# A graph network on one core: in the sort of the edges, ScalarE's copy of the running numbers is emitted one batch after VectorE's running sum

## Chip, cores and metric

The kernel runs on one core of one Trainium2 chip. The metric is the time of one execution on the device in microseconds; lower is better. A core has five engines with a queue each: PE (TensorE, matmuls; its weight loads are listed as PEld), DVE (VectorE), ACT (ScalarE), POOL (GpSimd) and SP (SyncE, which here issues the DMAs).

## What is computed

Two graph networks run one after the other on 6250 nodes with 128 features; the 206,250 edges (two directions of 100,000, and one loop for each node) come sorted by target. The first network gathers both ends of each edge, passes them through a small network and sums by target, in two layers. The second averages the neighbours, in three.

```python
for l in range(n_layers):                       # 2, first network
    m = jnp.concatenate([h[row], h[col]], axis=-1)
    m = jax.nn.relu(m @ msg_W1[l].T + msg_b1[l])
    m = m @ msg_W2[l].T + msg_b2[l]
    agg = jax.ops.segment_sum(m, col, num_segments=h.shape[0])
    upd = jnp.concatenate([h, agg], axis=-1) @ upd_W[l].T + upd_b[l]
    h = _layer_norm(h + upd, ln_g[l], ln_b[l])
...
for i in range(NUM_LAYERS):                     # 3, second network
    agg = jax.ops.segment_sum(h[src], dst, num_segments=n) * inv_deg
    h = agg @ Wl[i].T + bl[i] + h @ Wr[i].T
```

## The kernel before

Nodes are padded to 49 blocks of 128 (`NB`). Gathers and sums are matmuls with matrices of zeros and ones that are built on the chip.

**The sort.** For each target block `w`, the generator `sort(w)` takes a window of 36 x 128 edges and gives each edge of the block a place among 128 slots of its source block. It is cut into steps by `yield`; a `next` on the iterator `ahead` emits one step. The steps in order, with the lines of the profile:

1. load of the window `ed` (L333)
2. `key` (L336) and the one-hot `oh` over source blocks (L339), on VectorE
3. sums over quarters `half`, `four` (L343, L345) and the totals `tot` (L348), on VectorE
4. two small matmuls that give the start of each partition's count (L351, L352), and their copy by ScalarE into `four` (L353)
5. the running sum on VectorE (L356), then ScalarE's copy of it into the upper quarter of `upper` (L359) and VectorE's subtraction into the lower (L360)
6. `run` (L363 to L365), 7. `rank` (L368), 8. `fit`, `own`, `over`, `place` (L371 to L378), 9. `lo` and `v` (L384 to L386), all on VectorE
10. to 12. six `pick` tiles, two a step (helper L88, VectorE)
13. to 15. 36 matmuls of `pick` and `v` into the bank `so`, twelve a step (L398)
16. two copies of that bank by ScalarE, `sv` (L403) and `sv_f` (L405)
17. a transpose on TensorE (L408), ScalarE's copy `sv_t` (L410), and its store to the table `svd` in memory (L411)

That is 17 steps. `ed` has three buffers, `key` and `tot` two, and `oh`, `half`, `four`, `upper`, `run` and `v` one each.

**The loop around it.** In each of the two layers each target block is worked in 13 batches (`NI`) of four source blocks; the last batch holds source block 48 and the block's second part. In a batch `i` of layer 0 these are emitted, in this order:

- `fetch`, four batches ahead: a broadcast load `v_all` of a part of `svd[w]` (L430)
- the pending stores (L618): the one-hots to `ohd`, the counts to `cnt`
- `hot_first`, two batches ahead: VectorE builds `hot` (two operations, helper L88, three buffers) from `sv[w]` and `ot` (L442, four buffers) from `v_all`
- `picked`: 24 matmuls with `ot` into a `pe` bank (L501, L503), and ScalarE's `m` from it (L508)
- `widened`: ScalarE's `hd` from `hot` (L458)
- `settle`: the matmuls `agg` of the batch before (L521); after a block's last batch also the first step of `update`, which copies `agg` out by ScalarE (L530)
- `counts`: four matmuls into the one bank `pa` (L466), ScalarE's copy `ca` (L468), and in two batches of a block a further copy `kept` (L473, L480)
- a step of `update` of the block before, in every second batch (its last ones give `rest` at L210 and the matmul L232)
- one step of `ahead`, two in batches 2, 5, 8 and 11: 17 a block
- at batch 8 (`NI - 5`), as many steps more as it takes to have the next block's table `sv[w + 1]`
- at batch 7, `target_rows` of the next block: a matmul (L237), its sum `b` with a bias on VectorE (L239), and its split in three parts by ScalarE (L209) and VectorE (L210 to L212)

So in the steady state step 1 of a sort is emitted at batch 9 of one block, step 5 at batch 12, step 6 at batch 0 of the next block and steps 16 and 17 at batch 8. Dependencies and waits are put in by the framework, and each engine's instructions are laid out by it when the program is built.

Layer 1 has the same loop without `sort` and `counts`; the second network then works from the stored counts alone.

The lines that give a block its steps:

```python
                    for _ in range(2 if i % 3 == 2 else 1):
                        next(ahead, None)
                    while i == NI - 5 and l == 0 and w + 1 < NB and w + 1 not in sv:
                        next(ahead)
```

Of the kernel before, what the change touches and what calls it, by code (L numbers as in the profile page):

```python
# [67 lines left out]
def fast(tc, dram, ident, miss_i, x, src, dst, weights, columns, rows, out, edges):  # L68
# [12 lines left out]
    with ExitStack() as ctx:  # L81
# [247 lines left out]
        def sort(w):  # L329
# [24 lines left out]
            yield  # L354
            num, last = (four[:, x].rearrange("p k c -> p (k c)") for x in range(2))
            nc.vector.tensor_tensor_scan(last, num, num, 0.0, OP.add, OP.bypass)  # L356
            last = four[:, 1, :, 1:].rearrange("p k c -> p c k")
            upper = early.tile([128, H, NB], F16, name="upper", bufs=1)
            nc.scalar.copy(upper[:, Q:], last)  # L359
# [210 lines left out]
        def settle(most):  # L570

            nonlocal behind
            while len(pending) > most:
# [4 lines left out]
                if cols[-1] == NB:  # L578
# [3 lines left out]
                    next(behind)  # L582

        ahead = (None for w in range(NB) for _ in sort(w))
        while 0 not in sv:
            next(ahead)
# [345 lines left out]
```

## Time and profile before

| | |
|---|---|
| median of 3 runs | 4183.11 us (4173.44 to 4191.63) |
| the profiled execution's own time | 4183.25 us |
| its span, first to last instruction | 4181.5 us, TensorE's granted clock 0.987 |
| layer 0, from the first to the last running sum of the sort (L356) | 104.0 to 1896.9 us |
| TensorE busy in 400 to 800 us (layer 0) | 375.81 us of 400 |
| VectorE busy there | 337.26 us |
| ScalarE busy there | 252.46 us |
| running sum L356, copy L359, subtraction L360 | 1172, 989 and 949 ns, 49 of each |
| copies `sv` L403 and `sv_f` L405 | 621 and 569 ns, 49 of each |
| transpose L408, copy `sv_t` L410 | 276 and 277 ns |
| matmul L398 of the sort | 208 ns, 1764 of them, overlapped |

Durations of single instructions overlap with those of their neighbours on the same engine, so the distance from start to start is often less than the duration. In a line of the timeline the first two numbers are start and duration in us, then engine, line, operation, what it writes and reads, and in brackets the idle time of the engine before it and what ended it.

### The profile page before, as it was taken

How to read it: one execution, taken by the hardware profiler on the slowest of the kernel's cores; microseconds unless marked ns; L12 is line 12 of the kernel's file. 1: busy time of each engine (PE TensorE's matmuls, PEld its weight loads, DVE VectorE, ACT ScalarE, POOL GpSimd, SP SyncE). 2: the span in 40 equal slices, each digit the busy share in tenths (PEclk: the TensorE clock that was granted, in tenths of full speed). 3: DMA queues.
4: the chain of work that ended last, by engine and by line, in shares of the span. 5: the costliest groups of instructions: out<-in, count | busy, mean ns of one | idle time of the engine just before them, and what ended most of it. 6: DMA issues, size and time to landing. Idle time of an engine off the chain costs nothing. (4 is left out here: it accounts for less than half of the span.)

```text
span 4181.5 us, 118306 instructions
## 1 busy us (share of the span) xinstructions
PE 3971.0 (95%) x46833; PEld 3697.7 (88%) x46833; DVE 2935.0 (70%) x6941; ACT 2493.0 (60%) x4673; POOL 63.4 (2%) x59
## 2 busy tenths in 40 slices
PE   4899999999999999999999999999999999999998
PEld 2899999999999999999999999999999888888887
DVE  6888888888888888886777777777776444444443
ACT  4566666666666666666666666666665555555554
POOL 6000000000000000000000000000000000000000
PEclk8899999999999999999999999999999999999999
DMA  2455554555445545455666666666665444443554
GB/s 82 144 154 149 160 157 152 149 162 159 150 152 159 159 151 157 153 162 173 197 197 197 199 198 200 200 199 198 199 199 176 130 128 118 129 128 111 161 153 121
DMA packets 656082, 671.18 MB, mean 161 GB/s; under 512 B 113200, under 2 KB 504474, under 8 KB 655386
## 3 DMA queue, kind: packets, MB, share of 16 engines
q1 hardware_dynamic: 655514, 663.51, 53.0%
q8 instruction: 368, 6.03, 0.6%
q14 instruction: 200, 1.64, 0.1%
HBM read 534.28 MB, written 128.99 MB: 159 GB/s over the span
## 5 line engine op out<-in xcount | busy, mean ns | idle before, releaser
L501 PE MATMUL pe<-a,ot 128*128 128x128 bf16 x14700 | 1635.0, 221 | 1.5 <-DVE ot L442 1.4
L503 PE MATMUL pe<-b,ot 128*128 128x128 bf16 x14700 | 1631.2, 220 | 0.0
L501 PEld LDWEIGHTS <-ot 128*128 128x128 bf16 x14700 | 1033.9, 98 | 27.4 <-DVE ot L442 2.5
L503 PEld LDWEIGHTS <-ot 128*128 128x128 bf16 x14700 | 1037.5, 98 | 0.6
L695 PE MATMUL pe<-cf,h 128*128 128x512 f32 (+1 forms) x3822 | 926.5, 394 | 3.5 <-issue 1.9
L442 DVE TENSOR_SCALAR ot<-v_all,part 128x1024 bf16<-128x1024 bf16 (+1 forms) x1274 | 597.9, 472 | 321.7 <-PE pe L503 178.7
L695 PEld LDWEIGHTS pe<-cf,h 128*128 128x128 f32 x3822 | 676.1, 189 | 143.6 <-issue 2.0
L521 PE MATMUL agg<-m,hd 128*128 128x129 f32 x4900 | 694.6, 284 | 21.3 <-ACT agg_s L530 20.8
L689 ACT CAST cf<-c 128x2048 fp32r<-128x2048 uint8 (+2 forms) x253 | 433.6, 1714 | 340.7 <-PE pe L695 283.3
L521 PEld LDWEIGHTS agg<-m,hd 128*128 128x128 f32 x4900 | 603.8, 193 | 28.8 <-ACT agg_s L530 28.4
L88 DVE TENSOR_TENSOR hot<-sv,iota 128x512 bf16<-128x512 f16 (+1 forms) x1274 | 476.6, 410 | 147.1 <-ACT m L508 98.7
L512 ACT ACTIVATE m_r<-pe 128x512 fp32r<-128x512 f32 (+1 forms) x637 | 369.2, 580 | 338.3 <-PE pe L503 334.5
L689 DVE CAST cf<-c 128x2048 fp32r<-128x2048 uint8 (+2 forms) x254 | 280.7, 1105 | 358.2 <-PE pe L695 213.8
L458 ACT CAST hd<-hot 128x512 f32<-128x512 bf16 (+1 forms) x637 | 383.8, 602 | 219.3 <-PE agg L521 120.8
L508 ACT ACTIVATE m<-pe 128x512 f32<-128x512 f32 (+1 forms) x637 | 377.4, 592 | 222.8 <-PE pe L503 222.4
L513 DVE SCALAR_TENSOR_TENSOR m_r<-pe,m_r 128x512 fp32r<-128x512 f32 (+1 forms) x637 | 425.8, 669 | 67.5 <-ACT m_r L512 39.5
L521 PE MATMUL agg<-m_r,hd_r 128*128 128x256 f32 x2450 | 447.6, 303 | 1.4 <-DVE m_r L513 1.1
L489 ACT CAST hd_r<-hd_b 128x512 fp32r<-128x512 bf16 (+1 forms) x637 | 383.8, 603 | 22.3 <-PE agg L521 11.1
L468 ACT CAST ca<-pa 128x512 uint8<-128x512 f32 (+1 forms) x637 | 359.5, 564 | 1.6 <-PE pa L466 1.5
L521 PEld LDWEIGHTS agg<-m_r,hd_r 128*128 128x128 f32 x2450 | 331.9, 190 | 8.8 <-DVE m_r L513 1.6
L466 PE MATMUL pa<-hot 128*128 128x128 bf16 x2450 | 247.1, 221 | 92.9 <-ACT kept L480 90.1
L466 PEld LDWEIGHTS <-hot 128*128 128x128 bf16 x2450 | 193.7, 98 | 109.6 <-issue 101.5
(152 smaller groups left out, 2989.4 us busy)
## 6 DMA issues: line engine op xcount, KB each, us to landing
v_all<-svd SPq DMA_DIRECT2D x1176, 256.0 KB
c<-cnt SPq DMA_DIRECT2D x216, 512.0 KB
ohd<-hot SPq DMA_DIRECT2D x588, 128.0 KB
hd_b<-ohd SPq DMA_DIRECT2D x588, 128.0 KB
cnt<-ca SPq DMA_DIRECT2D x540, 64.0 KB
v_all<-svd SPq DMA_DIRECT2D x98, 128.0 KB
xw<-in_x SPq DMA_DIRECT2D x49, 64.0 KB
ohd<-hot SPq DMA_DIRECT2D x49, 64.0 KB
```

The costliest lines, as they stand in the source:

```text
L88: nc.vector.tensor_tensor(to, v.rearrange("p (r e) -> p r e", e=2).unsqueeze(2).to_broadcast([B, n, B, 2]), iota_2.unsqueeze(1).to_broadca ...
L442: nc.vector.tensor_scalar(t[:, :n].rearrange("p j k s -> p (j k) s"), v[:, :2 * n], part, None, op0=OP.is_equal)
L458: nc.scalar.copy(hd[:, :n].rearrange("p (r e) v -> p r e v", e=2), hot[:, 1, :n // 2].rearrange("p r v e -> p r e v"))
L466: nc.tensor.matmul(pa[:, j * B:(j + 1) * B], hot[:, 0, j // 2, :, j % 2], hot[:, 1, j // 2, :, j % 2], start=True, stop=True)
L489: nc.scalar.copy(hd[:, :n].rearrange("p (r e) v -> p r e v", e=2), h[:, :n * B].rearrange("p (r v e) -> p r e v", v=B, e=2))
L501: nc.tensor.matmul(pe[:, o], t[:, j, 0, :], a3[l][:, block, k, :], start=(k == 0), stop=False)
L503: nc.tensor.matmul(pe[:, o], t[:, j, 1, :], b3[:, k, :], start=False, stop=(k == 2))
L508: nc.scalar.activation(m[:, :n, :D], pe, AF.Relu)
L513: nc.vector.scalar_tensor_tensor(m[:, :n, 1, :], pe, 0.0, m[:, :n, 0, :].bitcast(F32), op0=OP.max, op1=OP.subtract)
L521: nc.tensor.matmul(agg[:, :F], hd[:, j, :], v, start=(c == 0), stop=(c == NB))
L689: (nc.scalar.copy if turn % 2 else nc.vector.tensor_copy)(cf[:, :k, :n].rearrange("p s w d -> p w s d"), c8[:, :n, s % R:s % R + k])
L695: nc.tensor.matmul(p[:, :n * B], h2[l % 2][:, s, k, :], cf[:, s % K, :n].rearrange("p w d -> p (w d)"), start=(s == 0 and k == 0), stop=(s ...
```

## The change

One `yield` is added in `sort`, between the running sum and its two readers. The running sum is then a step of its own, and ScalarE's copy and VectorE's subtraction come with the next `next`. The sort has 18 steps after it; the number of steps that the loop grants is not changed.

```diff
             num, last = (four[:, x].rearrange("p k c -> p (k c)") for x in range(2))
             nc.vector.tensor_tensor_scan(last, num, num, 0.0, OP.add, OP.bypass)
+            yield
             last = four[:, 1, :, 1:].rearrange("p k c -> p c k")
             upper = early.tile([128, H, NB], F16, name="upper", bufs=1)
             nc.scalar.copy(upper[:, Q:], last)
             nc.vector.tensor_sub(upper[:, :Q], last, half[:, Q:])
             yield
```

## The prediction

> **What bounds the kernel now.** I read the page's busy table first. TensorE is busy 95% of the span, so the first thought is that only TensorE's idle time can be won.
>
> ```profile
> PE 3971.0 (95%) x46833; PEld 3697.7 (88%) x46833; DVE 2935.0 (70%) x6941; ACT 2493.0 (60%) x4673; POOL 63.4 (2%) x59
> ```
>
> The sort runs only in layer 0 (scans L356 from 104.0 to 1896.9 us), so I then took the view of waits for 200 to 1900 us.
>
> ```profile
> DVE ot L442 <- DMA v_all<-svd: 120.4, 122, 3.4
> ACT upper L359 <- DVE four L356: 118.4, 45, 4.5
> PE pa L466 <- ACT kept L480: 88.8, 45, 3.1
> PE agg L521 <- ACT agg_s L530: 17.5, 32, 1.9
> ```
>
> The obvious reading: once per node block ScalarE stands 2.6 us (118.4/45) for the scan, the copies of pa behind it come late, the one pa bank stays full, and TensorE loses 88.8/45 = 1.97 us. The changed line is the head of that chain. Before pricing it at 2 us a block I asked what sets the period of a block, with VectorE's timeline of one block (scan ends at 954.83 and at 991.89).
>
> ```profile
> 953.66 1.17 DVE L356 TENSOR_TENSOR_SCAN four<-four 128x490 f16<-128x490 f16 x1
> ...
> 978.25 0.62 DVE L348 TENSOR_REDUCE tot<-four 128x49 f16<-128x441 f16 x1
> 978.77 0.48 DVE L442 TENSOR_SCALAR ot<-v_all,part 128x1024 bf16<-128x1024 bf16 x1
> 979.17 0.75 DVE L88 TENSOR_TENSOR hot<-sv,iota 128x512 bf16<-128x512 f16 x2
> 979.84 0.28 DVE L210 TENSOR_TENSOR rest<-mm,a 128x128 f32<-128x128 f32 x1
> 980.04 0.28 DVE L239 TENSOR_TENSOR b<-mm,row 128x128 f32<-128x128 f32 x1
> ...
> 987.89 0.49 DVE L442 TENSOR_SCALAR ot<-v_all,part 128x1024 bf16<-128x1024 bf16 x1 [1.44 <-DMA v_all<-svd]
> ...
> 990.32 0.49 DVE L442 TENSOR_SCALAR ot<-v_all,part 128x1024 bf16<-128x1024 bf16 x1 [0.33 <-DMA v_all<-svd]
> 990.72 1.17 DVE L356 TENSOR_TENSOR_SCAN four<-four 128x490 f16<-128x490 f16 x1
> ```
>
> The busy sums of the three stretches of that block (columns: stretch, length, PE, PEld, DVE, ACT, POOL, clock, DMA share, GB/s):
>
> ```profile
> 954.84:980.32 25.48, 23.74 (x341) 23.24 (x341) 25.45 (x62) 16.48 (x35) 0.00 (x0) 1.00 0.47 145
> 980.32:982.94 2.62, 2.62 (x41) 2.60 (x39) 2.08 (x9) 2.47 (x7) 0.00 (x0) 1.00 0.25 81
> 982.94:991.90 8.96, 8.79 (x127) 8.58 (x125) 4.48 (x11) 4.78 (x10) 0.00 (x0) 1.00 0.74 224
> ```
>
> There is a ring. From the end of a scan to the end of b L239 VectorE has 25.45 us of work in 25.48 us: no gap. Then ScalarE, which waits for that b, works off its queue, the sorted table is stored (svd L411) and the next block's broadcasts of it (v_all) land; VectorE waits for them at three ot (1.44, 0.45 and 0.33 us; the second stands in the left-out lines), and the scan stands behind the third. ScalarE and the store:
>
> ```profile
> 980.35 0.30 ACT L209 CAST b<-b 128x128 bf16<-128x128 f32 x1 [1.82 <-DVE b L239]
> ...
> 981.55 0.59 ACT L468 CAST ca<-pa 128x512 uint8<-128x512 f32 x1
> 982.03 0.28 ACT L410 CAST sv_t<-mm 100x128 bf16<-100x128 f32 x1
> ...
> 982.95 0.35 SPq L411 DMA_DIRECT2D svd<-sv_t  x1
> ```
>
> I took the same three marks for 46 blocks from the timeline: scan end to b end 25.49 us on average (25.3 to 26.2), b end to the svd issue 2.64 (2.62 to 2.94), svd issue to the next scan's end 9.61 (8.4 to 11.0, the loads' spread). The sum is the mean period, 37.75 us. TensorE has 35.16 us of work in the block shown: its 1.9 us stall is the slack of this ring, not its cause.
>
> **What the Trainium skill says.** "TensorE: Matmul & The Clock Gate", section "Architectural detail", has ScalarE's and VectorE's queues as strict FIFO; the trace agrees, since ca L468 of the last batch (pa ready at 989.89) runs at 992.82, behind upper L359. "Perfetto Trace Analysis", section "Optimization Strategy", says to find the gaps on the limiting engine and what ends them; taken alone that leads to the ScalarE wait, and here the gapless VectorE stretch decides. Its "Summary: the profiler window per engine type" says that a queue DMA's movement is outside its window: svd L411 shows 0.35 us, while the first ot that needs it starts 4.94 us after its issue.
>
> **The change, part by part.** No instruction is added or removed. The sort gets 18 steps where the loop grants 17 a block, so the `while` at batch NI-5 = 8 gives the missing one.
>
> 1. The copy L359 and the subtraction L360 are emitted a batch later. Each engine's order in the trace is not the order of emission but what was ready: key for the last block runs at 1806.1 us, its oh at 1878.6; L359 already stands ahead of ca L468 and kept L480, which are emitted before it. ScalarE has nothing else ready between m of the last batch (989.05) and that place, so I expect L359 to stay there. Gain 0. If it does move behind m and agg_s of the next batch, TensorE gets up to 1.97 + 17.5/45 = 2.4 us a block from its stalls, yet the ring holds no part of this wait, so again 0 in the sum. The last three blocks show it: there L359 runs behind kept (1898.11, wait 0.48) and their periods are 37.9 to 38.1. Bounds 0 and 2.1 us; I take 0.
>
> 2. The three groups of twelve matmuls L398 (0.70 us a group) go from batches 5, 6, 7 to 6, 7, 8. TensorE has no gap there, so they can't be pulled forward. It comes to the matmuls L232 and L237 for rest and b one group earlier, 0.7 us. What VectorE puts before rest is filling for the next block (oh, half, four, tot), taken while it had nothing better. With rest ready 0.7 us sooner, tot (0.62) and one ot (0.48) should fall behind b, where VectorE has 5.7 us idle a block. Gain in the 25.49 stretch: between 0 and 0.62 + 0.48 + 1.11 (four L345, at 977.10, too) = 2.2; I take 1.10.
>
> 3. sv and sv_f (L403, L405) cannot run before the last group now. Today they fill ScalarE's gap at 977.83, outside the ring; then they come after ca at 981.55. From its 982.14 end: both copies 0.7, the transpose L408 0.28 with the hand-overs about 0.15, sv_t 0.28, issue: near 983.5 instead of 982.95. Loss 0.55. The first block, which today makes up five steps at that batch, bounds it: matmuls end 150.08, svd at 152.50, that is 2.42; on the 982.14 above it gives 984.5, loss 1.6. Lower bound 0.3, if SP's wait behind ohd (982.53) swallows part. TensorE's transpose stands behind the copy, and the matmuls of batch 9 behind it: about 1 us of stall, paid out of the 1.9 us of slack. If that slack were gone, it would cost that 1 us.
>
> 4. SP issues the same DMAs; svd L411 passes at most one cnt and one ohd store (0.34, 0.38). The v_all loads follow svd by the same 9.61, as the scan stays behind the third ot. Bounds: 0.49 + 0.33 = 0.8 gain if that ot falls behind the scan, 0.4 loss if another store goes first. I take 0.
>
> 5. run, rank, v and picks also move a batch. They stay in the gapless stretch, whose sum does not change by order. Picks end about 971.7 for a group at 973.6 then: covered.
>
> Sum a block: -1.10 + 0.55 = -0.55 us. Some 47 periods: -26 us. The profiled execution (span 4181.5, its time 4183.25) becomes 4157; the median shown is 4183.11, so it is 4157 there too. Layer 1 and the matrix stage have no sort.
>
> **Rivals.**
> A, gain and loss cancel (rest comes only 0.5 us earlier, or ScalarE's delay is 1.1): 4183 - 5 = 4178. For: TensorE's stall has been shown to be slack. Against: two opposite parts would have to be equal.
> B, slower: the svd tail. The copies, the transpose and the store come into the ring and nothing leaves the gapless stretch. At 0.3 to 1.6 a block, say 0.9: 47 x 0.9 = 42, 4225. It decides as soon as less than 0.55 us of filling goes behind b. For: the first block's 2.42 us tail. Against: L237 does come a group earlier.
> C, the plain reading: ScalarE's wait goes and VectorE's ring loosens as well (L360 and run behind the hot tiles, third ot behind the scan), so that TensorE's work bounds: 35.16 + 0.45 against 37.75, 2.1 us x 47 = 100, 4083. For: 118.4 us of waits in plain sight. Against: the last three blocks.
> That the order on ScalarE does not change at all is part of the forecast.
>
> **How the numbers follow.** Forecast (4130 to 4170) 0.40, of which 0.02 lies within 0.5%; A 0.23, B 0.28, C 0.09. Range: C's nearest part and the ends of step 2 (-2.2 + 0.3 = -1.9 x 47 = -89, 4094) to B's upper middle (+1.1 x 47 = 52, 4235): 4094 to 4235; the forecast's own is 4130 to 4170. 0.5% is 21 us, about what a measurement can tell from no change: faster 0.38 + 0.09 = 0.47, same 0.02 + 0.23 = 0.25, slower 0.28.
>
> **What would show it.** Right: L359 still ahead of the last ca with a wait near 2.5 us; groups L398 in batches 6 to 8; fewer fillings before rest; scan to b near 24.4, b to svd near 3.2, svd to scan near 9.6. Wrong: L359 without a wait and TensorE's L466 stall gone with a shorter period (C), scan to b still 25.5 (B), or a tail over 4 us.

## The result, and the profile after

The kernel after the change takes 4218.41 us (median of 5 runs, 4210.31 to 4220.93), the kernel before 4183.11 us. The ratio is 1.0082 with a 95% interval of 1.0061 to 1.0104: slower, and the whole interval lies above the 0.5% that the prediction took for what a measurement can tell from no change. Forecast was 4157. The profiled execution has a span of 4208.5 us (4181.5 before) and a granted clock of 0.991 (0.987).

The page's busy table looks as before; the work is the same.

```profile
PE 3964.9 (94%) x46833; PEld 3684.6 (88%) x46833; DVE 2931.5 (70%) x6941; ACT 2503.0 (59%) x4673; POOL 63.2 (2%) x59
```

The view of waits for 200 to 1900 us, the layer with the sort (us in total, times, longest):

```profile
PE mm L409 <- ACT sv_f L406: 74.3, 44, 2.2
ACT upper L360 <- DVE four L356: 70.6, 42, 3.1
...
DVE ot L443 <- DMA v_all<-svd: 62.3, 81, 1.9
...
PE pa L467 <- ACT kept L481: 42.7, 43, 2.4
...
PE agg L522 <- ACT agg_s L531: 23.3, 40, 1.1
```

Lines below the new `yield` have moved by one. ScalarE's wait for the scan fell from 118.4 to 70.6 us and TensorE's wait at `pa` from 88.8 to 42.7 us. A reader who stops there would call the change a success. In their place stands a wait that was not there, 74.3 us at the transpose L409, and the whole is longer.

The periods say where. I measured the same marks in 45 blocks of each timeline, in us after the end of a scan L356 (means):

| | before | after |
|---|---|---|
| period, scan end to scan end | 37.74 | 38.45 |
| second matmul group for b, L237, ends | 23.35 | 22.72 |
| b L239 starts on VectorE | 25.21 | 25.23 |
| VectorE ends the hot pair (two `hot` operations in a row) that feeds the next `ohd` store | 27.69 | 27.70 |
| VectorE's idle time up to there | 0.15 | 0.21 |
| transpose starts | 25.73 | 27.99 |
| `sv_t` ready | 27.56 | 28.61 |
| store `svd` issued | 28.14 | 28.66 |
| from there to the end of the next scan | 9.60 | 9.78 |
| the third ot on the new table, the last before the scan, starts | 36.17 | 36.25 |
| from its start to the start of that scan | 0.40 | 1.02 |
| TensorE's idle time in a period | 2.38 | 3.19 |

The period grew by 0.70 us: 0.52 up to the store and 0.18 behind it. Over 47 periods that is 33 us, against the 34 us that the ratio gives (0.0082 x 4183). The two profiled executions themselves differ by 27.0 us: from the first to the last scan the changed one is 31.8 us longer, and the rest of it is 4.8 shorter.

Now one block of the changed kernel (its scan ends at 585.10). VectorE's timeline:

```profile
608.75 0.62 DVE L348 TENSOR_REDUCE tot<-four 128x49 f16<-128x441 f16 x1
609.27 0.76 DVE L88 TENSOR_TENSOR hot<-sv,iota 128x512 bf16<-128x512 f16 x2
609.94 0.30 DVE L210 TENSOR_TENSOR rest<-mm,a 128x128 f32<-128x128 f32 x1
610.14 0.29 DVE L239 TENSOR_TENSOR b<-mm,row 128x128 f32<-128x128 f32 x1
...
611.86 0.75 DVE L88 TENSOR_TENSOR hot<-sv,iota 128x512 bf16<-128x512 f16 x2
615.26 0.49 DVE L88 TENSOR_TENSOR hot<-sv,iota 128x256 bf16<-128x256 f16 x2 [2.65 <-PE pa L467]
...
621.31 0.48 DVE L443 TENSOR_SCALAR ot<-v_all,part 128x1024 bf16<-128x1024 bf16 x1 [1.04 <-DMA v_all<-svd]
621.72 0.75 DVE L88 TENSOR_TENSOR hot<-sv,iota 128x512 bf16<-128x512 f16 x2
622.39 1.17 DVE L356 TENSOR_TENSOR_SCAN four<-four 128x490 f16<-128x490 f16 x1
```

tot still stands ahead of rest and b: nothing left the gapless stretch. And the stretch does not end at b; it goes on to the hot pair at 611.86, and only behind that comes the first real gap (2.65 us). At the other end a hot pair has come between the third ot and the scan, which stood back to back before. In the kernel before, the pair stood ahead of the third ot, where VectorE waits for that ot's load anyway. Two lines of VectorE's timeline of before, in the block that the prediction shows: the pair that the `ohd` store ahead of `svd` waits for, and the pair ahead of the third ot (990.32).

```profile
981.75 0.76 DVE L88 TENSOR_TENSOR hot<-sv,iota 128x512 bf16<-128x512 f16 x2
...
989.23 0.76 DVE L88 TENSOR_TENSOR hot<-sv,iota 128x512 bf16<-128x512 f16 x2
```

The two rows of the table on the third ot give the weight of this. The store is 0.52 us later, but the third ot only 0.08: its distance from the store shrank by 0.44. From the third ot to the scan 0.62 us were added; the pair stands there in 39 of the 45 blocks, and in none before. So 0.52 - 0.44 + 0.62 is the 0.70.

ScalarE's timeline of the tail in the changed kernel, then SP's:

```profile
610.47 0.30 ACT L209 CAST b<-b 128x128 bf16<-128x128 f32 x1 [2.78 <-DVE b L239]
...
611.67 0.59 ACT L469 CAST ca<-pa 128x512 uint8<-128x512 f32 x1
612.15 0.61 ACT L404 CAST sv<-so 128x100 f16<-128x100 f32 x1
612.28 0.56 ACT L406 COPY sv_f<-so 128x100 f32<-128x100 f32 x1
613.25 0.27 ACT L411 CAST sv_t<-mm 100x128 bf16<-100x128 f32 x1 [0.41 <-PE mm L409]
```

```profile
610.06 2.90 SPq L619 DMA_DIRECT2D ohd<-hot  x2
613.39 0.32 SPq L619 DMA_DIRECT2D cnt<-ca  x1
613.81 0.34 SPq L412 DMA_DIRECT2D svd<-sv_t  x1
615.49 0.81 SPq L431 DMA_DIRECT2D v_all<-svd  x2
```

sv and sv_f have come behind ca, as predicted. But SP's queue tells a second story. The second of the two `ohd` stores on the first line is issued 0.03 us after the hot pair is done (612.61), then comes a `cnt` store, then `svd`. In the kernel before SP's lines at that place are:

```profile
982.53 0.32 SPq L618 DMA_DIRECT2D ohd<-hot  x1
982.95 0.35 SPq L411 DMA_DIRECT2D svd<-sv_t  x1
983.35 0.34 SPq L618 DMA_DIRECT2D cnt<-ca  x1
983.78 0.38 SPq L618 DMA_DIRECT2D ohd<-hot  x1
984.44 0.79 SPq L430 DMA_DIRECT2D v_all<-svd  x2
```

There `svd` is right behind the `ohd`, although `sv_t` was done at 982.31; one store has changed places with it. In all 45 blocks the entry just ahead of `svd` is an `ohd` before and a `cnt` after. Behind `svd` the stores have moved as well: a `cnt` and an `ohd` stood between it and the first load before, and in 41 of 45 blocks none does after. The first load is issued 1.62 us after `svd` instead of 1.85.

### The profile page after: what moved, and what is told of

Same layout as the page of the kernel before. It is cut to its first block, busy times and chain, and to the rows that moved or that the text cites. A ratio compares the mean times of both kernels' runs of the same rounds, so it can differ in the third digit from the quotient of the medians.

```text
span 4208.5 us, 118345 instructions
## 1 busy us (share of the span) xinstructions
PE 3964.9 (94%) x46833; PEld 3684.6 (88%) x46833; DVE 2931.5 (70%) x6941; ACT 2503.0 (59%) x4673; POOL 63.2 (2%) x59
## 3 DMA queue, kind: packets, MB, share of 16 engines
q14 instruction: 200, 1.64, 0.1%
```

## The experiments

Two theories at first. The tail theory: the loss is the moved tail (sv, sv_f, transpose, sv_t), and the copy that gives the change its name is neutral. The rival: the later copy and subtraction themselves delay run, picks and matmuls. Later a third had to be formed, on SP's queue. Ratios are to the kernel before, with their 95% intervals; marks are means over 45 blocks as above.

**The copy a batch later, the tail where it was.** Base: the changed kernel. A second step is granted in batch 0 as well, so the sort again has its steps and the matmul groups are at batches 5 to 7.

```diff
-                    for _ in range(2 if i % 3 == 2 else 1):
+                    for _ in range(2 if i % 3 == 2 or i == 0 else 1):
```

> The changed kernel with 18 steps granted to a block (two in batch 0), so that the copy and the subtraction are still emitted one batch after the running sum, but the matmul groups, the copies sv and sv_f and the store svd are back in batches 5 to 8. Tail theory (what costs is the tail of the sort, now behind batch 8): about 4183, b end to svd back at 2.6 us, scan to b 25.5, period 37.7. Copy theory (what costs is the later place of the copy, the subtraction and run): about 4218, period 38.4.

Measured: 4182.05 us, ratio 1.0004 (0.9997 to 1.0011). Period 37.67, `svd` at 28.12, no hot pair between the third ot and the scan in any block. ScalarE's wait for the scan is 2.61 us a block, about as before, so the shorter wait of the changed kernel came with the tail too. The change in its own words costs nothing and brings nothing.

**The tail a batch later, the copy where it was.** Base: the kernel before, with the `yield` put ahead of the matmul loop of the sort.

```diff
+            yield
             for c in range(C):
                 nc.tensor.matmul(ps[:, :2 * NK], picks[c // Q][:, c % Q // 2, :, c % 2], halves[:, c, :],
```

> The kernel before with an empty step ahead of the sort's matmul groups, so that only groups, copies, transpose and store come one step later; running sum, copy and subtraction stay in one step. Tail theory: about 4216, b end to svd 3.1 us, TensorE waits some 1.7 us a block at the transpose. Copy theory: about 4183.

Measured: 4222.03 us, ratio 1.0100 (1.0084 to 1.0117). Period 38.52, `svd` at 28.62, TensorE's wait at the transpose 1.70 us a block; the hot pair stands ahead of the scan in 39 of 45 blocks, as in the changed kernel. The tail alone brings the whole loss. What is in the tail was still open: ScalarE's part should shrink if ScalarE has less to do there.

**b's first copy on VectorE** (edit V; the copy L209 of the split of b alone), on the kernel before and on the changed one:

```diff
-        def split(to, p):
+        def split(to, p, head=None):
...
-            nc.scalar.copy(to[:, 0], p)
+            (head or nc.scalar.copy)(to[:, 0], p)
...
-            split(t, b)
+            split(t, b, nc.vector.tensor_copy)
```

> The kernel before with the first part of the split of b copied by VectorE instead of ScalarE, so that ScalarE no longer waits for VectorE's backlog at batch 8. Ring theory (scan, gapless VectorE, b, ScalarE, svd, v_all, scan sets the period): svd no longer hangs on b, the store is issued 1.3 to 1.8 us earlier against the scan, the period falls from 37.75 to about 36.3, 4183 - 1.4 x 47 = 4117. TensorE theory (the period is TensorE's work and its stall behind upper, whatever b does): 4183 within 10.

> The same edit on the changed kernel. Ring theory: sv and sv_f follow the last matmul group without waiting for b, svd is issued 1.5 us earlier, TensorE's wait at the transpose falls from 1.7 to about 0.3 us a block; about 4120, and the distance to the same edit on the kernel before is under 15. If the changed kernel's loss came from elsewhere in VectorE's order, it would stay 35 above that one.

Measured: before with V 4183.14 us, ratio 1.0005 (0.9998 to 1.0012); changed kernel with V 4220.96 us, ratio 1.0093 (1.0076 to 1.0109). Both expectations missed. The edit did its part: `sv_t` is ready at 26.95 instead of 27.56 on the one, at 27.71 instead of 28.61 on the other, and on the changed kernel TensorE's wait at the transpose falls from 1.69 to 0.70 us. But `svd` is issued at 28.17 and 28.68, where it was. ScalarE's and SP's timelines of the changed kernel with V (two views):

```profile
691.20 0.27 ACT L411 CAST sv_t<-mm 100x128 bf16<-100x128 f32 x1 [0.41 <-PE mm L409]
```

```profile
691.62 0.32 SPq L619 DMA_DIRECT2D ohd<-hot  x1
692.03 0.38 SPq L619 DMA_DIRECT2D cnt<-ca  x1
692.50 0.37 SPq L412 DMA_DIRECT2D svd<-sv_t  x1
```

The table is ready at 691.47 and its store goes a microsecond later, behind the other two. So the tail theory as I had it falls: with a shorter tail, something else holds the store. Third theory: the store is behind the hot pair of VectorE by way of SP's queue (hot pair 27.7, `ohd` 0.03 after it, each further store 0.43 to 0.50).

**`svd` issued from ScalarE's queue** (edit S), alone and with V, on both kernels. This takes SP's queue out of the path to the store.

```diff
-            nc.sync.dma_start(svd[w], t)
+            nc.scalar.dma_start(svd[w], t)
```

> The kernel before with one edit: the store of the sorted table (svd) is issued from ScalarE's queue, right behind the copy sv_t that fills it, instead of from SP's. Queue theory (in the kernel before the store stands in SP's queue behind an ohd store that waits for VectorE's hot pair; sv_t itself is ready at 27.56 us after the scan, the store goes at 28.14): the store goes near 27.65, 0.5 us earlier, and if the rest of the ring follows, 0.5 x 47 = 24 us are gained: 4159. ScalarE theory (the ring runs through ScalarE's tail, as the prediction had it): the store already goes as soon as sv_t is there, so nothing moves: 4183. A third outcome, 4183 with the store earlier, would say that the v_all loads, which stay in SP's queue, then stand behind that ohd store instead.

> The same edit on the changed kernel. There sv_t ends at 28.61 us after the scan and the store goes at 28.66, with an ohd and a cnt store just ahead of it in SP's queue. Tail theory (sv, sv_f, transpose, sv_t after the last matmul group hold the store): no change, 4218. Queue theory alone (the extra cnt store ahead of svd is the loss): the store goes 0.4 to 0.5 us earlier, 4195 to 4200.

> The changed kernel with both edits: the first copy of b's split goes to VectorE (sv_t was at 27.71 us with it) and svd is issued from ScalarE's queue. Two-path theory (ScalarE's tail and SP's queue end together at 28.6, so that lifting one gives nothing and lifting both gives the smaller): the store goes near 27.8, 0.85 x 47 = 40 us less, 4178. If neither path is what holds the ring (for example the v_all loads wait for something else on SP), 4218 stays.

> The kernel before with both edits. sv_t was at 26.95 us with the first one, so the store can go near 27.0 instead of 28.14. Two-path theory: up to 1.1 x 47 = 52 us less, 4131; as the scan stands behind the third ot, whose v_all load stands in SP's queue behind ohd, a part of it can be lost: 4131 to 4160. If the loads behind SP's stores hold the ring: 4183.

| | time | ratio | `sv_t` ready | `svd` issued | `svd` to scan end | period |
|---|---|---|---|---|---|---|
| before + S | 4179.25 | 0.9987 (0.9977 to 0.9997) | 27.53 | 27.56 | 9.88 | 37.44 |
| before + V + S | 4172.40 | 0.9961 (0.9947 to 0.9975) | 26.90 | 26.93 | 10.35 | 37.28 |
| changed + S | 4221.81 | 1.0080 (1.0063 to 1.0097) | 28.64 | 28.67 | 9.86 | 38.53 |
| changed + V + S | 4185.83 | 0.9999 (0.9990 to 1.0008) | 27.63 | 27.66 | 9.91 | 37.57 |

On the changed kernel (4218 and 4178 were expected of S and of V + S) V alone gives nothing, S alone gives nothing, and both together bring it back to the time before the change: two paths end at the same moment, and each holds the store without the other. One is ScalarE and TensorE (sv_t at 28.6); the other is VectorE's hot pair and two stores in SP's queue (27.70 + 0.03 + 0.43 + 0.50 = 28.66). ScalarE's timeline of the changed kernel with both edits:

```profile
678.01 0.27 ACT L411 CAST sv_t<-mm 100x128 bf16<-100x128 f32 x1 [0.41 <-PE mm L409]
678.30 0.28 ACTq L412 DMA_DIRECT2D svd<-sv_t  x1
```

The store now follows its copy at once. With V and S on the changed kernel it goes 1.00 us earlier (27.66 for 28.66) and the period is 0.88 us shorter (37.57 for 38.45), while the hot pair stays ahead of the scan in 41 of 45 blocks: there the store's time is what the period follows. The store is also 0.48 us earlier than in the kernel before, yet the times are the same: the third ot is 0.79 earlier than there (35.38 for 36.17), and the hot pair ahead of the scan takes 0.61 of that back.

On the kernel before, S moves the store by 0.58 us, so there SP's queue alone held it: 27.69 + 0.03 + 0.43 = 28.15, measured 28.14. About half came through to the period of the profiled execution (0.30); it is the fastest of twelve, and the medians (4179.25 and 4185.44 side by side) give 0.13 a block. The loads `v_all` still stand behind `ohd` and `cnt` in SP's queue, but that is not where the rest was lost: the third ot starts at 35.25 instead of 36.17, 0.92 us earlier. It was lost behind that ot. With this edit, too, the layout puts the hot pair between the third ot and the scan (41 of 45 blocks), and the distance is 1.01 instead of 0.40. 4179 came where 4159 would have been the full amount. V + S on the kernel before shows the same: the store goes 1.21 us earlier, the third ot 1.08, the period is 0.46 us shorter, and 4172 is outside the 4131 to 4160 expected. No run takes the pair away alone.

**The next block's b a batch earlier** (edit E), on the kernel before: what step 2 of the prediction had counted on, made by hand.

```diff
-                    if i == NI - 6 and (l, w) != (1, NB - 1):
+                    if i == NI - 7 and (l, w) != (1, NB - 1):
```

> The kernel before with the next block's b (target_rows) emitted one batch earlier, which puts rest and b ahead of tot, own and key on VectorE: what step 2 of the prediction thought the change would do by itself. If an earlier b is worth what the prediction put on it: b ends 1.1 us or more earlier after the scan (24.4 or less) and the period shortens by the same, 4131. Queue theory (in the kernel before the store svd stands in SP's queue behind an ohd store, that waits for the hot pair at the end of VectorE's stretch, not for b): b earlier, hot pair and svd where they were (28.1), 4183 within 0.3%.

Measured: 4169.37 us, ratio 0.9974 (0.9962 to 0.9985). VectorE's timeline, then SP's:

```profile
784.96 0.28 DVE L210 TENSOR_TENSOR rest<-b,b 128x128 f32<-128x128 f32 x1
785.16 0.61 DVE L348 TENSOR_REDUCE tot<-four 128x49 f16<-128x441 f16 x1
...
788.32 0.76 DVE L88 TENSOR_TENSOR hot<-sv,iota 128x512 bf16<-128x512 f16 x2
```

```profile
789.10 0.32 SPq L618 DMA_DIRECT2D ohd<-hot  x1
789.52 0.34 SPq L411 DMA_DIRECT2D svd<-sv_t  x1
```

tot has gone behind b, and b ends at 22.37 instead of 25.49 after the scan, 3.1 us earlier. The hot pair ends at 27.48 instead of 27.69, and `svd` goes at 27.96 instead of 28.14. Of 3.1 us, 0.18 reaches the store and 0.27 the period. The stretch holds the same work in another order, and the store waits for its last member.

**The upper copy on GpSimd**, on the kernel before: ScalarE then has no wait for the scan at all.

```diff
-            nc.scalar.copy(upper[:, Q:], last)
+            nc.gpsimd.tensor_copy(upper[:, Q:], last)
```

> The kernel before with the copy of the running numbers (upper, the moved line) done by GpSimd instead of ScalarE, so that ScalarE has no wait for the scan in its queue at all. Stall theory (rival C of the prediction: TensorE's 2.0 us a block at pa, behind ScalarE's wait for the scan, set the time): 2 us x 47 = 94 us less, 4090. Ring theory (the period is VectorE's gapless stretch, then the store svd, then its loads; TensorE's stall is slack): 4183 within 0.3%, with TensorE's stall at pa smaller and standing elsewhere. If GpSimd's copy is slow enough to delay VectorE's run behind it: somewhat over 4183.

Measured: 4242.01 us, ratio 1.0151 (1.0128 to 1.0175), the last of the outcomes named and more of it than "somewhat". The one-line views of the two halves of upper, of this kernel (copy L359, subtraction L360) and then of the kernel before (subtraction; least, median and longest ns):

```profile
L359 POOL COPY upper<-four x5: 987/1092/1096, 828.8 to 984.9; 128x441 f16<-128x441 f16 x5
```

```profile
L360 DVE TENSOR_TENSOR upper<-four,half x5: 937/1662/1666, 829.0 to 985.1; 128x441 f16<-128x441 f16 x5
```

```profile
L360 DVE TENSOR_TENSOR upper<-four,half x3: 949/950/953, 918.4 to 992.2; 128x441 f16<-128x441 f16 x3
```

The copy is hardly slower than ScalarE's 989 ns (the profile's spans on GpSimd are rough), but VectorE's subtraction beside it takes 1.66 us in most blocks (mean 1.48 over 43) instead of the 0.95 that it takes beside ScalarE's copy. The hot pair ends at 28.63, 0.94 later, and `svd` at 29.08, 0.94 later. TensorE's waits in 200 to 1900 us:

```profile
PE agg L521 <- ACT agg_s L530: 129.8, 44, 4.0
...
PE pa L466 <- ACT kept L480: 4.3, 8, 1.0
```

The wait at `pa` is gone (88.8 before), and one at `agg` has taken its place (17.5 before). So this run does not refute the stall theory cleanly, since the stall moved instead of going. The stall at `pa` went and the kernel became slower, but the slower subtraction could hide a gain. Of the 1.24 us by which the period is longer (38.98), 0.94 stand up to the hot pair, and the store is later by the same amount.

**Two faster versions.** V + S + E on the kernel before, and V + S with the `ohd` and `cnt` stores of the loop issued from GpSimd's queue (L618):

```diff
-                        nc.sync.dma_start(*stores.pop(0))
+                        nc.gpsimd.dma_start(*stores.pop(0))
```

> The kernel before with three edits: b a batch earlier, the first copy of its split on VectorE, svd issued from ScalarE's queue. Neither b nor SP's queue stands ahead of the store then. Ring theory: the store goes before 26.9 us (its time in the run without the earlier b), and the period is held by the loads v_all, which still stand behind an ohd and a cnt store in SP's queue: period 36.8 to 37.3 us, 4140 to 4172. If the gapless stretch alone decided: no better than the run without the earlier b, 4172.

> The kernel before with the first copy of b's split on VectorE, svd issued from ScalarE's queue, and the ohd and cnt stores of the node blocks issued from GpSimd's queue, so that SP's queue holds the loads v_all alone. Queue theory: with the stores gone, the loads go as soon as svd is written; svd at 26.9 and the loads 0.4 us nearer to it: period 36.6 to 37.0, 4130 to 4150. Against: GpSimd's queue may issue more slowly (a store's buffer comes free later, and pa's copies wait for it), then 4180 or more.

Measured: 4159.64 us, ratio 0.9946 (0.9929 to 0.9963), and 4157.97 us, ratio 0.9942 (0.9926 to 0.9959). Both beat the kernel before and the changed one. The time of the first fell into its range, but not by the way named: `svd` went at 27.39, not before 26.9, since `sv_t` came later there (27.36), and the period is 37.19. In the second, `svd` goes at 26.43 and SP's queue holds loads alone, yet the scan ends 10.53 us behind it, so the period is 36.96, at the upper end of what was expected and 8 us above it in time. The timeline says where that time goes: the third ot on the new table starts at 34.15, 2.0 us earlier than in the kernel before, but in all 45 blocks a hot pair and a fourth ot stand between it and the scan, which starts 1.64 us later.

## Why the prediction was wrong

The step that failed is step 2, with the term -1.10 us a block. The sum was -0.55 and +0.70 was measured; of the 1.25 us between them this term is 1.10, and the sign hung on it.

- **Step 1** (the copy stays where it is in ScalarE's queue, gain 0): right. upper still stands ahead of the last ca, and the copy a batch later alone measured a ratio of 1.0004. Its wait is 1.7 us (70.6/42), though, where 2.5 was named as the sign.
- **Step 2** (matmuls for b a group earlier; tot and one ot fall behind b; -1.10): the first half is right, L237 ends 0.63 us earlier (forecast 0.7). The conclusion is wrong twice. VectorE had not been waiting for that matmul: it ended 1.86 us before b started (23.35 and 25.21 in the kernel before), so its coming earlier released nothing. I had read the work ahead of rest as filling taken for want of rest; the timeline of before, with no idle time ahead of rest, says that rest was in a queue; its operand came sooner, and its place in the queue stayed (tot is ahead of rest in all 45 blocks of both kernels). And even with tot behind b, as edit E made it, 3.1 us of earlier b gave 0.27 us of period. b was not the end of the stretch. Measured: 0 in place of -1.10 (scan to the end of b 25.49 before and 25.51 after).
- **Step 3** (the tail comes into the ring, +0.55): right in size for the store, 0.52, and TensorE's stall at the transpose is 1.69 us where about 1 was said, paid from slack as said (2.38 us of idle time before, of which the part at `pa` shrank from 1.99 to 0.98). But half of the cause was missing: the tail holds the store together with SP's queue, and shortening it alone gives nothing back.
- **Step 4** (SP's queue, 0, with 0.4 of loss "if another store goes first" as its bound): the bound happened. A `cnt` store goes ahead of `svd`, 0.50 us. It adds nothing to the 0.52 because it ends at the same moment as the tail. Behind the store, 0.18 us was lost where 0 was said. The step took the scan to stay right behind the third ot. The timeline shows two parts of opposite sign instead: the third ot 0.44 us nearer to the store, and 0.62 us more from it to the scan, with the hot pair in between. No run isolates them.
- **Step 5** (run, rank, v, picks move at no cost): right; VectorE's idle time up to the hot pair stays at 0.2 us.
- **The ring itself**: right that TensorE's and ScalarE's big waits were slack (the two fell by 46 and 48 us in layer 0 while the kernel became slower) and that the period is a gapless VectorE stretch, a store and its loads. Wrong in a link: between VectorE and the store stood SP's queue (hot pair, `ohd`, `svd`), not ScalarE, which had 0.6 us to spare (sv_t 27.56, store 28.14).

With 0, +0.52 and +0.18 in place of -1.10, +0.55 and 0, the sum is +0.70 us and 47 periods give 4216. Rival B, that the tail comes into the ring and nothing leaves the gapless stretch, is what happened; it gave 4225 and had 0.28.

The Trainium skill, in "DMA: Bandwidth & Descriptors", section "Issuing engines are not separate DMA queues", says that issuing from several engines saves only the issue time, usually small beside the transfer. The runs here agree for the larger part and show one thing more. Of the 0.58 us by which leaving SP's queue moved `svd`, 0.43 is the `ohd` store's own turn, from its issue to the next. The other 0.15 is its wait for the hot pair (`ohd` at 27.71, table ready at 27.56), which `svd` shared because it stood behind it. With V the table is ready at 26.95 and the `ohd` goes at 27.75, so that this wait is 0.80.

## What to carry to other kernels

When a gapless stretch sets a period, find its true last member: look at the store or load that closes the ring, read the queue it is issued from, and ask what the entry ahead of it waits for. An operand that comes earlier gains nothing where its reader is not idle before it; check that with one subtraction in the timeline (operand ready, reader starts) before counting on it. And a step inserted early in a hand-staged pipeline moves everything behind it, so the last steps, nearest to the consumer, are where the bill comes: granting one more step brought the time back to 1.0004. Then follow the gain to the next link: in every run here that issued the store from ScalarE's queue, VectorE had a hot pair between the third ot and the scan in 41 or all of the 45 blocks, and it took 0.6 us or more.

## What the runs showed of the hardware that was not expected

- A VectorE subtraction of 128x441 f16 took 0.95 us beside a ScalarE copy from the same source and 1.66 us, in most blocks, beside a GpSimd copy from it; the GpSimd copy took 1.09 us. In 12 of 44 blocks it was the other way round: the subtraction took 0.95 us and the copy 1.43. "GPSIMD Engine Reference" in the Trainium skill, section "1. Specifications", has GpSimd's access to SBUF shared with VectorE and names VectorE instructions with two SBUF inputs, as this one has, as a case of contention; the trace agrees.
- A store that is merely queued ahead cost 0.43 to 0.50 us on SP from issue to issue, more than the 0.32 to 0.38 us that its own line shows.
